# A vision-mamba pair on one core: stage openings, idle half units and turned sequences of the side work are rearranged

## The chip, the core and the metric

The kernel runs on one core of a Trainium2 chip. The metric is the time of one execution on the device, in microseconds (us). An engine's name is written as in the profile: PE (TensorE), DVE (VectorE), ACT (ScalarE), POOL (GpSimd), SP (SyncE, here the queue from which all DMAs are issued).

## The reference, cut to what matters

Eight images of 64 x 64 tokens with 192 channels go through two layers.

Layer 0 projects 192 channels to 2 x 384, applies a depthwise 3 x 3 convolution and silu to one half, runs a state-space scan over the tokens in two orders (along rows and along columns), gates the result with silu of the other half, projects back, adds the input, and adds an MLP (192 to 768 to 192).

Layer 1 splits the 192 channels in two halves. The left half goes through three convolutions. The right half is normalized, projected to 192 + 192, convolved depthwise, and scanned in four directions with 16 states per channel:

```python
def step(h, t):
    u_t, d_t, b_t, c_t = t
    h = jnp.exp(d_t[..., None] * A) * h + (d_t * u_t)[..., None] * b_t[:, :, None, :]
    return (h, jnp.einsum('bkdn,bkn->bkd', h, c_t))
scan_in = (jnp.moveaxis(xs4, -1, 0), jnp.moveaxis(delta, -1, 0), jnp.moveaxis(Bs, -1, 0), jnp.moveaxis(Cs, -1, 0))
...
_, ys = lax.scan(step, h0, scan_in)
ys = jnp.moveaxis(ys, 0, -1) + Ds[None, :, :, None] * xs4
...
yv = _ln(yv, out_norm_g, out_norm_b) * jax.nn.silu(z)
xr_out = jnp.einsum('bhwe,ce->bhwc', yv, out_proj_w)
```

Two of the four directions walk the tokens column by column ("turned" sequences), so a transposed copy of the scan's input is needed. The four results are added, normalized, gated and projected; both halves are interleaved and added to the layer's input.

## The kernel before, in words

The spine of the kernel is `selective_scan`, layer 1's scan. It runs 3072 units, 384 for each image. A unit is a tile of 128 rows (8 channels x 16 states) and 1024 tokens. For each unit SP fetches the decay's exponents (`fetch`, L1430, 512 KB, issued 6 units ahead), ACT takes their exponential (`decay`, L1435), PE spreads the input term over the states (`spread`, L1443), DVE multiplies by B (`weigh`, L1458) and scans (`scan`, L1465), POOL multiplies by C (L1467), ACT carries the last column on (L1473, L1474), and every fourth unit PE sums the states (`gather`, L1485). Each engine runs its instructions in the order in which the program emits them; `pin` keeps that order.

All other work runs beside the scan, in stages. They are Python generators, queued for each image: while image b is scanned, `conv0`, `ssd` and `mlp0` (layer 0) of image b+1 are emitted, then `conv_branch` with `scan_sums` as its side work and `scan_outputs` (end of layer 1) of image b-1, then `scan_inputs` and `transposed` (the inputs of the scan) of image b+1. Each unit has two halves, and in each half `Beside.half` emits some side work. A generator yields the cost of each piece in a rough unit, or `None`: wait for the next half. The credit rule is

```python
self.credit = min(self.credit, self.rate) + self.rate
while self.credit > 0.0 and self.stages:
    for cost in self.stages[0]:
        if cost is None:
            return
        self.credit -= cost
        if self.credit <= 0.0:
            return
    self.stages.pop(0)
```

and the rate is set once for each image from the sum of costs, the number of halves, and a reserve of 13 halves per stage (`spread_over`). Halves in which a stage only yields `None` are called empty here. The scan's own PE work also spends credit. What a stage has not emitted when its image's scan is about to end is emitted at once (`finish`); in both kernels nothing is left over there.

At its opening a stage loads what it needs. In `conv0` these are the first row of tokens, the projection weights `w_in`, the first block (`load(0)`), three parts of the convolution's diagonal weights (`diag`, L482), the projection `xp` (L486) and the second block. The second block is loaded twice, by two calls of `load(1)` into the same buffers; the second load is queued behind the first one's landing. `mlp0` loads `w_z`, the block's five tiles, `w_out` and `w1` before its first `gate`. `conv_branch` loads both convolutions' weights (L957), `scan_inputs` its two `diag` tiles (before the first `mean`). `ssd` opens with the steps of `group(0)`: loads, then POOL, ACT, POOL, PE and ACT, POOL in turn, with empty halves between them. `transposed` reads whole sequences (`whole`, L1100), copies each quarter with rows and columns exchanged on ACT (`part`, L1110), and stores it (L1117).

`stages(0)` runs before the scan with no scan beside it (the prologue), and the last image's sums and outputs run after it (the tail).

Of the kernel before, what the change touches and what calls it, by code (L numbers as in the profile page):

```python
# [9 lines left out]
F32 = mybir.dt.float32  # L10
# [7 lines left out]
L = HH * WW  # L18
# [271 lines left out]
def pause(n):  # L290

    for i in range(n):
        yield None


def among(gen, calls):

    calls = list(calls)
    for n, cost in enumerate(gen):
        yield cost  # L300
        if n % 2 == 1 and calls:
            calls.pop(0)()
    for call in calls:
        call()
        yield None
# [72 lines left out]
def conv0(cx, x):  # L378
# [3 lines left out]
    with cx.pool("cw0") as wp, cx.pool("v0", 2) as vp:  # L382
# [95 lines left out]

        pads = [wp.tile([128, R2 + 2, PW], F32, tag=f"pad{j}", name=f"pad{j}") for j in range(NJ)]
        diag = wp.tile([128, NJ, 9, 64], F32, tag="diag", name="diag")  # L480
        for j in range(NJ):
            pin(nc.sync.dma_start(out=diag[:, j], in_=k["diag0"][:, j]))  # L482
            yield None
        xp = wp.tile([128, 2 * NJ, 2 * NP0], F32, tag="xp0", name="xp0")
        for i in range(2):
            pin(nc.sync.dma_start(  # L486
                out=xp[64 * i : 64 * (i + 1)], in_=k["p0_xp"].rearrange("(j p) k m -> p j (k m)", p=64)
            ))
        yield from pause(2)
        for j in range(NJ):  # L490
            pin(nc.gpsimd.memset(pads[j], 0.0))
        yield from pause(2)
        load(1)
        yield from pause(2)
        load(1)
        for j in range(NJ):
            yield from project(0, j)
        for p in range(NP):
            for j in range(NJ):
                yield from convolve(p, j)  # L500
# [10 lines left out]
def ssd(cx):  # L511
# [15 lines left out]
    with cx.pool("g0", 2) as gp, cx.pool("s0", 2) as sp:  # L527
# [49 lines left out]
            groups[g] = both, over, *(t.rearrange(by_chunk, k=K2) for t in (dt, da, upto, toend))  # L577

        coming = group(0)
        for n in (8, 2, 2, 3, 2):  # L580
            next(coming)
            yield from pause(n)
        next(coming, None)
# [131 lines left out]
def mlp0(cx, x, x1):  # L715
# [9 lines left out]
    with cx.pool("mw0") as wp, cx.pool("m0", 2) as mp:  # L725
# [27 lines left out]
        def add(i):  # L753
            for y0, y1 in ys[i]:
                pin(nc.gpsimd.tensor_add(y0, y0, y1))
# [91 lines left out]
        w_out = wp.tile([128, NJ, C], F32, tag="w_out", name="w_out")  # L847
        w2 = wp.tile([128, NF, C], F32, tag="w2", name="w2")
        yield from load_split(cx, w_z, k["p0_w_in"][:, INNER0:])
        for call in loads(0):  # L850
            call()
            yield None
        pin(nc.sync.dma_start(out=w_out, in_=k["p0_w_out"].rearrange("(j p) m -> p j m", p=128)))
        yield None
        yield from load_split(cx, w1, k["p0_w1"])
        yield from gate(0)
        add(0)
        pin(nc.sync.dma_start(out=w2, in_=k["p0_w2"].rearrange("(f p) m -> p f m", p=128)))
        yield from turn(0)
        yield from project(0)  # L860
        for call in loads(1):
            call()
            yield None
        for i in range(1, NI + 1):
            if i < NI:
                yield from gate(i)
# [9 lines left out]
def conv_branch(cx, xl, short, out, side=None):  # L876

    nc, pin, k = cx.nc, cx.pin, cx.k
    with cx.pool("cw1") as wp, cx.pool("a1", 2) as ap:

        pads = [[wp.tile([CH, RB + 2, PW], F32, tag=f"p{c}{i}", name=f"p{c}{i}") for i in range(2)] for c in range(2)]
        xs, ys, os, shs, ws = {}, {}, {}, {}, []

        def conv(ps, pad, w):
            for t, (dy, dx) in enumerate(TAPS):
# [65 lines left out]
            yield 0.0  # L951

        load(0)
        for n in ("conv1_w", "conv2_w"):
            w = wp.tile([CH, 9, CH], F32, tag=n, name=n)
            for r in range(3):
                pin(nc.sync.dma_start(out=w[:, 3 * r : 3 * (r + 1)], in_=k[n][:, 3 * r : 3 * (r + 1)]))  # L957
                yield None
            ws.append(w)
# [50 lines left out]
def scan_inputs(cx, xr, xn, u):  # L1010
# [4 lines left out]
    with cx.pool("dw") as wp, cx.pool("b1", 2) as bp:  # L1015
# [71 lines left out]
        yield from in_turn(range(NB), mean, norm, project, wait, wait, convolve, store)  # L1087


def transposed(cx, u):  # L1090

    nc, pin = cx.nc, cx.pin
    with cx.pool("t1") as tp:
        wholes = []
        for n, src in enumerate((u[0], u[2][0:64])):
            wholes.append(tp.tile([src.shape[0], L], F32, tag=f"whole{n}", name=f"whole{n}"))

        def load(n, q):
            here = slice(q * L // 4, (q + 1) * L // 4)
            pin(nc.sync.dma_start(out=wholes[n][:, here], in_=(u[0], u[2][0:64])[n][:, here]))  # L1100

        for q in range(4):
            load(0, q)
            yield from pause(1 if q < 3 else 3)
        front = []
        for whole, dst in zip(wholes, (u[1], u[2][64:128])):
            for q in range(4):
                w0 = q * WW // 4
                part = tp.tile([whole.shape[0], L // 4], F32, tag="part", name="part", bufs=3)
                pin(nc.scalar.copy(part.rearrange("p (w h) -> p w h", h=HH), wh(whole)[:, w0 : w0 + WW // 4, :]))  # L1110
# [4 lines left out]
                yield None  # L1115
# [72 lines left out]
def scan_outputs(cx, y, xn, short, out):  # L1188
# [3 lines left out]
    with cx.pool("e1", 2) as ep:  # L1192
# [65 lines left out]
class Beside:  # L1258
# [465 lines left out]
```

## Time and profile before

| | us |
|---|---|
| median of 3 runs | 16537.61 (16530.31 to 16537.72) |
| the profiled execution's own time | 16556.29 |
| its span, first to last instruction | 16554.4 |
| prologue, to the first scan | 913 |
| image 0's scan | 1792 |
| image 1's and image 2's scan | 2004 and 2014 |
| image 7's scan | 1570 |
| tail | 264 |

The lower rows are read from the trace of the profiled execution by the start of each image's first scan instruction. All engines work in all of these stretches except the tail. In the profile a line such as L1465 is the line of the kernel that emitted the instruction, `h<-dA,carry,dB` names what it writes and reads, and the numbers behind the bar are busy us, mean ns of one, and idle us of the engine just before, with what ended it.

### The profile page before, as it was taken

How to read it: one execution, taken by the hardware profiler on the slowest of the kernel's cores; microseconds unless marked ns; L12 is line 12 of the kernel's file. 1: busy time of each engine (PE TensorE's matmuls, PEld its weight loads, DVE VectorE, ACT ScalarE, POOL GpSimd, SP SyncE). 2: the span in 40 equal slices, each digit the busy share in tenths (PEclk: the TensorE clock that was granted, in tenths of full speed). 3: DMA queues.
4: the chain of work that ended last, by engine and by line, in shares of the span. 5: the costliest groups of instructions: out<-in, count | busy, mean ns of one | idle time of the engine just before them, and what ended most of it. 6: DMA issues, size and time to landing. Idle time of an engine off the chain costs nothing.

```text
span 16554.4 us, 220424 instructions
## 1 busy us (share of the span) xinstructions
PE 13560.5 (82%) x75752; PEld 4803.7 (29%) x75752; DVE 12258.6 (74%) x9264; ACT 9901.5 (60%) x17354; POOL 10649.1 (64%) x5765
## 2 busy tenths in 40 slices
PE   8977887788977888888888789887898878878876
PEld 4423322332223321333213332233322333211111
DVE  2268888886778766887678876788767887778994
ACT  3365677565674656647566475665657556655653
POOL 3258766875568655686557865577655775566773
PEclk9987888889788896888878898788887889877766
DMA  3288878888787887888778878888778887788884
GB/s 90 84 218 198 214 196 227 194 209 202 182 226 192 202 208 184 222 193 207 205 195 208 199 199 207 206 202 198 196 195 212 200 209 203 193 224 201 214 209 125
DMA packets 1605044, 3248.22 MB, mean 196 GB/s; under 512 B 390536, under 2 KB 841752, under 8 KB 1603928
## 3 DMA queue, kind: packets, MB, share of 16 engines
q1 hardware_dynamic: 1603928, 3234.12, 78.5%
q8 instruction: 605, 9.91, 0.3%
q14 instruction: 511, 4.19, 0.1%
HBM read 2555.20 MB, written 678.18 MB: 195 GB/s over the span
## 4 chain that ended last, share of the span: by engine, by line
PE 41%; DMA 17%; DVE 16%; ACT 11%; POOL 8%; issue 5%; SPq 2%; DVEq 0%; POOLq 0%; ACTq 0%
DVE h L1465 9%; PE ps_cv L343 7%; DMA dA<-dld 5%; PE acc L1485 4%; DVE dB L1458 4%; PE ps_c L886 4%; POOL h L1467 3%; PE dB L1443 2%; ACT dA L1435 2%; PE ps_m L795 2%; PE ps_sum L1178 2%; PE ps_xp L1355 2%; DMA dus<-dud 2%; PE ps_y L686 1%; PE ps_var L1000 1%
## 5 line engine op out<-in xcount | busy, mean ns | idle before, releaser
L1467 POOL TENSOR_TENSOR h<-h,bc 128x1023 f32<-128x1023 f32 x3072 | 7229.2, 2354 | 4661.0 <-DVE h L1465 4123.4
L1465 DVE TENSOR_TENSOR_SCAN h<-dA,carry,dB 128x1024 f32<-128x1024 f32 x3072 | 7201.5, 2344 | 712.6 <-ACT dA L1435 224.1
L1458 DVE TENSOR_TENSOR dB<-dB,bc 128x1024 f32<-128x1024 f32 x3072 | 3742.3, 1218 | 1921.2 <-PE dB L1443 1909.4
L1435 ACT ACTIVATE dA<-dA,neg_a 128x1024 f32<-128x1024 f32 x3072 | 3505.9, 1141 | 44.2 <-DMA dA<-dld 39.1
L1485 PE MATMUL acc<-h,gather 128*32 128x512 f32 x12288 | 2310.3, 721 | 524.3 <-ACT h L1474 230.7
L1443 PE MATMUL dB<-dus,spread 24*128 24x512 bf16 x6144 | 1379.8, 434 | 849.4 <-DVE h L1465 764.0
L1490 ACT COPY y<-acc 128x512 f32<-128x512 f32 x1536 | 883.3, 575 | 944.0 <-PE acc L1485 818.5
L886 PE MATMUL ps_c<-p,conv_w 96*96 96x512 f32 x2304 | 1242.8, 668 | 70.2 <-ACT p L906 63.2
L1443 PEld LDWEIGHTS <-spread 24*128 24x128 bf16 x6144 | 309.6, 93 | 3099.6 <-issue 1452.3
L1473 ACT COPY carry<-h 128x1 f32<-128x1 f32 x3072 | 573.0, 187 | 947.5 <-DVE h L1465 944.4
L686 PE MATMUL ps_y<-dtx,M 64*64 64x64 f32 x12288 | 784.9, 258 | 333.6 <-DVE Hn L677 309.4
L1474 ACT ACTIVATE h<-h,bc 128x1 f32<-128x1 f32 x3072 | 905.2, 295 | 158.7 <-ACT carry L1473 3.0
L343 PE MATMUL ps_cv<-pad,diag 64*64 64x512 f32 x6912 | 835.6, 603 | 6.4 <-ACT y L1490 5.4
L686 PEld LDWEIGHTS ps_y<-dtx,M 64*64 64x64 f32 x12288 | 662.5, 169 | 492.7 <-issue 311.4
L1485 PEld LDWEIGHTS acc<-h,gather 128*32 128x32 f32 x12288 | 304.6, 117 | 1535.5 <-issue 938.2
L107 ACT ACT_TABLE_LOAD x577 | 740.3, 1283 | 10.2
L618 PE MATMUL ps_d<-R,after 128*128 128x384 f32 x1024 | 565.0, 642 | 72.5 <-POOL R L594 26.9
L613 ACT COPY bc<-ps_t 64x256 f32<-64x256 f32 x256 | 93.4, 365 | 855.9 <-PE ps_t L608 855.6
L886 PEld LDWEIGHTS ps_c<-p,conv_w 96*96 96x96 f32 x2304 | 368.5, 177 | 777.8 <-issue 686.8
L1355 PE MATMUL ps_xp<-u,xp 128*108 128x512 f32 x768 | 474.4, 706 | 98.9 <-DMA u<-u 86.1
L1394 POOL TENSOR_TENSOR du<-dl,u 128x1024 f32<-128x1024 f32 x192 | 452.2, 2355 | 127.0 <-ACT dl L1391 127.0
L373 PE MATMUL ps_h<-oa,w1a 128*128 128x256 f32 x1536 | 451.5, 414 | 58.6 <-ACT h L826 17.3
(243 smaller groups left out, 19239.9 us busy)
## 6 DMA issues: line engine op xcount, KB each, us to landing
dA<-dld SPq DMA_DIRECT2D x3072, 512.0 KB
dud<-terms SPq DMA_DIRECT2D x192, 768.0 KB
dus<-dud SPq DMA_DIRECT2D x2304, 64.0 KB
bc<-bcd SPq DMA_DIRECT2D x256, 512.0 KB
y<-yrows SPq DMA_DIRECT2D x256, 384.0 KB
u<-u SPq DMA_DIRECT2D x192, 512.0 KB
dld<-dl SPq DMA_DIRECT2D x192, 512.0 KB
y<-y SPq DMA_DIRECT2D x3072, 32.0 KB
```

Source lines behind the costliest of these rows:

```text
L343: pin(nc.tensor.matmul(ps[64 * b : 64 * (b + 1)].rearrange("p (h w) -> p h w", w=WW), lhsT=diag[:, t, :], rhs=pad[64 * i : 64 * (i + 1), b ...
L686: pin(nc.tensor.matmul(psy[d][here, h * HP : (h + 1) * HP], lhsT=M[here, d, h, :], rhs=dtx[here, d, h, :], start=True, stop=d == 1,))
L886: pin(nc.tensor.matmul(ps.rearrange("p (h w) -> p h w", w=WW), lhsT=w[:, t, :], rhs=pad[:, dy : dy + RB, dx : dx + WW], start=t == 0, stop ...
L1355: pin(nc.tensor.matmul(ps[:NXP], lhsT=k["xp"][:, g, t, :], rhs=u_of[m][t][:, here], start=t == 0, stop=t == 2))
L1435: pin(nc.scalar.activation(dAs[q], dAs[q], AF.Exp, scale=k["neg_a"][:, steps[m][1], t, i : i + 1]))
L1443: pin(nc.tensor.matmul(dBs[q][:, half, :], lhsT=k["spread"][at : at + 3 * UD, :], rhs=du_of[n][at : at + 3 * UD, i // 2, :], start=True, s ...
L1458: pin(nc.vector.tensor_mul(dBs[q], dBs[q], of(q)[0]))
L1465: pin(nc.vector.tensor_tensor_scan(order(h, g), order(dA, g), order(dB, g), carry, ALU.mult, ALU.add))
L1467: pin(nc.gpsimd.tensor_mul(h[:, rest], h[:, rest], C_[:, rest]))
L1474: pin(nc.scalar.activation(end, end, AF.Identity, scale=C_[:, last : last + 1]))
L1485: pin(nc.tensor.matmul(ps[32 * v : 32 * (v + 1)], lhsT=k["gather"], rhs=hs[q - 3 + v][:, here], start=True, stop=True))
L1490: pin(nc.scalar.copy(y[:, here], ps))
```

## The change

- `among` gets a parameter `n`: a call is made after every n-th piece (it was every second).
- `conv0` loads only the first part of `diag` ahead of its first pieces. The other two parts and `xp` are loaded among the first projections, one after each piece. The doubled `load(1)` is a single one, behind those projections. Fewer empty halves.
- `ssd` opens with 7, 1, 1, 2, 1 empty halves in place of 8, 2, 2, 3, 2.
- `mlp0` starts `gate(0)` when x and half of y are loaded. The rest of y and `w_out` come among its pieces, `w1` after it, and `w2` among the pieces of `project(0)` with the next block.
- `conv_branch` loads the second convolution's weights among its first pieces.
- `scan_inputs` loads its `diag` tiles among its first pieces, and has 4 empty halves for 6; `scan_outputs` has 4 for 6.
- `transposed` copies two quarters in each half in place of one, with four `part` buffers in place of three, and starts one half earlier.
- The reserve in `spread_over` is 9 halves per stage in place of 13.

```diff
-def among(gen, calls):
+def among(gen, calls, n=2):
     calls = list(calls)
-    for n, cost in enumerate(gen):
+    for i, cost in enumerate(gen):
         yield cost
-        if n % 2 == 1 and calls:
+        if i % n == n - 1 and calls:
             calls.pop(0)()
...
# conv0
-        for j in range(NJ):
+        def load_diag(j):
             pin(nc.sync.dma_start(out=diag[:, j], in_=k["diag0"][:, j]))
-            yield None
-        xp = wp.tile([128, 2 * NJ, 2 * NP0], F32, tag="xp0", name="xp0")
-        for i in range(2):
...
+        load_diag(0)
         yield from pause(2)
         for j in range(NJ):
             pin(nc.gpsimd.memset(pads[j], 0.0))
-        yield from pause(2)
+        yield from pause(1)
+        for j, calls in enumerate(([lambda: load_diag(1)], [lambda: load_diag(2)], [load_xp])):
+            yield from among(project(0, j), calls, 1)
         load(1)
-        yield from pause(2)
-        load(1)
-        for j in range(NJ):
-            yield from project(0, j)
...
# ssd
-        for n in (8, 2, 2, 3, 2):
+        for n in (7, 1, 1, 2, 1):
...
# mlp0
-        for call in loads(0):
-            call()
-            yield None
-        pin(nc.sync.dma_start(out=w_out, in_=k["p0_w_out"].rearrange("(j p) m -> p j m", p=128)))
+        first, *calls = loads(0)
+        first()
...
+        calls.pop(0)()
         yield None
+        calls.pop(0)()
+        yield from pause(2)
+        yield from among(gate(0), calls + [load_out], 1)
+        yield None
+        add(0)
         yield from load_split(cx, w1, k["p0_w1"])
-        yield from gate(0)
-        add(0)
-        pin(nc.sync.dma_start(out=w2, in_=k["p0_w2"].rearrange("(f p) m -> p f m", p=128)))
         yield from turn(0)
-        yield from project(0)
-        for call in loads(1):
-            call()
-            yield None
+        yield from among(project(0), loads(1) + [load_2], 1)
...
# conv_branch
+        for r in range(3):
+            load_w(0, r)
+            yield None
         load(1)
...
-        yield from in_turn(range(NB), scale, first, wait, second, third, add, store)
+        turns = in_turn(range(NB), scale, first, wait, second, third, add, store)
+        yield from among(turns, [lambda r=r: load_w(1, r) for r in range(3)])
...
# scan_inputs
-            pin(nc.sync.dma_start(out=diag[n], in_=k["diag_" + n]))
-            yield from pause(2)
-        yield from pause(2)
+        yield from pause(4)
...
+        yield from among(turns, [
+            lambda n=n: pin(nc.sync.dma_start(out=diag[n], in_=k["diag_" + n])) for n in "ab"
+        ])
...
# transposed
-            yield from pause(1 if q < 3 else 3)
+            yield from pause(1 if q < 3 else 2)
...
-                part = tp.tile([whole.shape[0], L // 4], F32, tag="part", name="part", bufs=3)
+                part = tp.tile([whole.shape[0], L // 4], F32, tag="part", name="part", bufs=4)
...
-                yield 1.0
-                yield None
+                if q % 2 == 1:
+                    yield 1.0
+                    yield None
...
# scan_outputs
-                yield from pause(6)
+                yield from pause(4)
...
# Beside.spread_over
-        self.rate = own / halves + work / (halves - 13 * len(self.stages))
+        self.rate = own / halves + work / (halves - 9 * len(self.stages))
```

More of the change, by code (lines that the diff above doesn't have):

```diff
@@ L480, in conv0, with load_xp @@
         diag = wp.tile([128, NJ, 9, 64], F32, tag="diag", name="diag")
-        for j in range(NJ):
+        xp = wp.tile([128, 2 * NJ, 2 * NP0], F32, tag="xp0", name="xp0")
+        def load_diag(j):
             pin(nc.sync.dma_start(out=diag[:, j], in_=k["diag0"][:, j]))
-            yield None
-        xp = wp.tile([128, 2 * NJ, 2 * NP0], F32, tag="xp0", name="xp0")
-        for i in range(2):
-            pin(nc.sync.dma_start(
-                out=xp[64 * i : 64 * (i + 1)], in_=k["p0_xp"].rearrange("(j p) k m -> p j (k m)", p=64)
-            ))
+        def load_xp():
+            for i in range(2):
+                pin(nc.sync.dma_start(
+                    out=xp[64 * i : 64 * (i + 1)], in_=k["p0_xp"].rearrange("(j p) k m -> p j (k m)", p=64)
+                ))
+        load_diag(0)
         yield from pause(2)
@@ L849, in mlp0, with load_out, load_2 @@
         yield from load_split(cx, w_z, k["p0_w_in"][:, INNER0:])
-        for call in loads(0):
-            call()
-            yield None
-        pin(nc.sync.dma_start(out=w_out, in_=k["p0_w_out"].rearrange("(j p) m -> p j m", p=128)))
-        yield None
+        first, *calls = loads(0)
+        first()
+        def load_out():
+            pin(nc.sync.dma_start(out=w_out, in_=k["p0_w_out"].rearrange("(j p) m -> p j m", p=128)))
+        def load_2():
+            pin(nc.sync.dma_start(out=w2, in_=k["p0_w2"].rearrange("(f p) m -> p f m", p=128)))
+        calls.pop(0)()
+        yield None
+        calls.pop(0)()
[3 more added lines that the diff above has]
+        add(0)
         yield from load_split(cx, w1, k["p0_w1"])
-        yield from gate(0)
-        add(0)
-        pin(nc.sync.dma_start(out=w2, in_=k["p0_w2"].rearrange("(f p) m -> p f m", p=128)))
         yield from turn(0)
-        yield from project(0)
-        for call in loads(1):
-            call()
-            yield None
+        yield from among(project(0), loads(1) + [load_2], 1)
         for i in range(1, NI + 1):
@@ L881, in conv_branch @@
         pads = [[wp.tile([CH, RB + 2, PW], F32, tag=f"p{c}{i}", name=f"p{c}{i}") for i in range(2)] for c in range(2)]
-        xs, ys, os, shs, ws = {}, {}, {}, {}, []
+        xs, ys, os, shs = {}, {}, {}, {}
         def conv(ps, pad, w):
@@ L953, in conv_branch, with load_w @@
         load(0)
[L954 to L957, printed above, removed]
-                yield None
-            ws.append(w)
+        ws = [wp.tile([CH, 9, CH], F32, tag=n, name=n) for n in ("conv1_w", "conv2_w")]
+        def load_w(i, r):
+            here = slice(3 * r, 3 * (r + 1))
+            pin(nc.sync.dma_start(out=ws[i][:, here], in_=k[("conv1_w", "conv2_w")[i]][:, here]))
+        for r in range(3):
+            load_w(0, r)
+            yield None
         load(1)
@@ L1086, in scan_inputs @@
                 pin(nc.gpsimd.memset(pads[n][i], 0.0))
-        yield from in_turn(range(NB), mean, norm, project, wait, wait, convolve, store)
+        turns = in_turn(range(NB), mean, norm, project, wait, wait, convolve, store)
+        yield from among(turns, [
+            lambda n=n: pin(nc.sync.dma_start(out=diag[n], in_=k["diag_" + n])) for n in "ab"
+        ])
 def transposed(cx, u):
@@ L1113, in transposed @@
                     load(1, q)
-                yield 1.0
-                yield None
+                if q % 2 == 1:
+                    yield 1.0
+                    yield None
                 if len(front) == 2:
```

## The prediction

> **What bounds the kernel now.** I read the page's engine rows first. TensorE (PE) is busy 82%, VectorE 74% and the 16 DMA engines 78.5%: no engine is full, so the limits differ by stage. One scan unit costs VectorE 2344 + 1218 ns (rows L1465, L1458), so no unit can take under 3.56 us.
>
> ```profile
> span 16554.4 us, 220424 instructions
> ...
> PE 13560.5 (82%) x75752; PEld 4803.7 (29%) x75752; DVE 12258.6 (74%) x9264; ACT 9901.5 (60%) x17354; POOL 10649.1 (64%) x5765
> ...
> q1 hardware_dynamic: 1603928, 3234.12, 78.5%
> ...
> L1465 DVE TENSOR_TENSOR_SCAN h<-dA,carry,dB 128x1024 f32<-128x1024 f32 x3072 | 7201.5, 2344 | 712.6 <-ACT dA L1435 224.1
> L1458 DVE TENSOR_TENSOR dB<-dB,bc 128x1024 f32<-128x1024 f32 x3072 | 3742.3, 1218 | 1921.2 <-PE dB L1443 1909.4
> ```
>
> Second, the busy times by stretch, cut at the borders of the stages that run beside image 2's scan, and one stretch of the last image with no side work. The columns are the stretch, its length, busy us of PE, PE loads, VectorE, ScalarE, GpSimd, then granted clock, DMA share and GB/s.
>
> ```profile
> 4610.00:4914.00 304.00, 270.84 (x1916) 100.05 (x1914) 250.29 (x142) 221.75 (x412) 199.22 (x100) 0.93 0.91 231
> 4914.00:5461.00 547.00, 418.43 (x4000) 193.04 (x4000) 452.85 (x449) 263.25 (x503) 455.49 (x287) 0.80 0.80 189
> ...
> 5901.00:6196.00 295.00, 270.16 (x753) 75.31 (x750) 187.58 (x107) 139.80 (x255) 164.33 (x90) 0.95 0.85 218
> 6196.00:6361.00 165.00, 144.27 (x288) 30.61 (x286) 111.57 (x91) 119.16 (x186) 95.17 (x50) 0.65 0.69 167
> 6361.00:6563.00 202.00, 185.71 (x760) 43.74 (x762) 153.34 (x99) 133.54 (x226) 113.04 (x59) 0.76 0.73 183
> 6563.00:6613.00 50.00, 17.76 (x52) 2.04 (x46) 24.63 (x15) 31.10 (x37) 22.96 (x11) 0.53 0.87 245
> ...
> 6624.00:6665.00 41.00, 27.56 (x78) 8.07 (x78) 24.88 (x15) 14.58 (x29) 21.28 (x12) 0.67 0.96 220
> ...
> 15975.00:16290.00 315.00, 169.26 (x556) 25.29 (x552) 301.76 (x175) 181.05 (x336) 232.95 (x102) 0.62 0.80 192
> ```
>
> In order: conv0, ssd, conv_branch, scan_outputs, scan_inputs, transposed, the opening of the next conv0, bare scan. The same stretches restricted to L1465 hold 71, 96, 53, 25, 41, 7, 7 and 87 scans, so a unit takes 4.28, 5.70, 5.57, 6.60, 4.93, 7.14, 5.86 and 3.62 us. The reader is to see three things. Bare scan runs at VectorE's bound. conv_branch (PE 92% busy) and conv0 (89%) are at TensorE. The two stretches around the image change have TensorE below 70% and DMA at 0.87 and 0.96: they wait for transfers.
>
> Third, the chain of waits in the 120 us around that image change (start, length, what):
>
> ```profile
> 6579.37 15.45 DMA dA<-dld
> 6596.64 7.02 DMA whole<-u
> 6603.81 1.99 ACT part L1110
> ...
> 6619.77 8.18 DMA dud<-terms
> 6627.96 10.40 DMA w_inb<-in_w_in_dram
> 6638.43 5.77 DMA dA<-dld
> ...
> 6650.08 8.73 DMA diag<-diag
> 6658.84 10.27 DMA y<-y
> ```
>
> Transfers end these waits, one of them the diag load that the change moves.
>
> **The change, part by part.** I sum against the profiled execution, 16556.29 us with 16554.4 of span. That is 18.7 us (0.11%) above the median of 16537.61; I carry the sum over as a difference.
>
> *(A) Fewer empty halves, smaller reserve (13 to 9 per stage).* I walked the credit rule of `half` through all 6144 halves with both sets of yields. Opening halves in which a stage issues no compute fall: conv0 12 to 6, ssd 16 to 11, mlp0 9 to 4, conv_branch 6 to 3, scan_outputs 5 to 3, scan_inputs 5 to 3. The rate falls too, 2.305 to 2.231 credits a half. So the work does not close up much: halves per stage are conv0 143 to 144, ssd 192 to 189, mlp0 175 to 175, conv_branch 107 to 106, scan_outputs 50 to 48, scan_inputs 81 to 80, transposed 14 to 9, idle before the next image 6 to 17. Halves that spend no credit at all: 224 to 221 of 768. What is saved at the openings is handed back as a longer idle end. Upper bound of the gain, if each unit keeps its stage's pace and the freed ones run at 3.6: 1.5 x 2.1 (ssd) + 0.5 x 1.97 + 1 x 3.0 + 0.5 x 1.33 - 0.5 x 0.68 (conv0) = 7.5 us an image. Lower bound 0: the same matmuls must pass a TensorE that is 90% busy. I take the middle, 4 us, x 6 images: -24.
>
> *(B) The doubled load(1) of conv0 goes.* Before issues xa (512 KB) and two xb (64 KB) twice into the same buffers, the second time queued on SP behind the landing of the first. 640 KB at the 231 GB/s of that stage is 2.8 us, with DMA 91% busy. Seven conv0 stages run beside a scan: -20. In the first one (94 GB/s, no scan) it is free.
>
> *(C) Two diag loads and xp go behind the first projections.* 2 x 288 KB + 430 KB = 1.0 MB leave the stretch at 0.96 DMA share. 7 scans took 41 us there against 25 at 3.6: 16 us lost, 8.73 of them in the chain under diag. The bytes return under conv0 at 0.91, so the bounds are 0 and -16; I take -7, x 7: -49. The earlier end of transposed (8.5 units before the image switch, where 3 were) is the same slack, not counted again.
>
> *(D) Turned sequences in pairs.* Eight L1110 copies take 1.94 us each on ScalarE. Two per half instead of one leaves their sum, 15.6 us; ScalarE's scan work meanwhile (dA 1142, two carry pieces 183 and 295, y and terms, some 2.75 a unit) is only spread over fewer units. The first copy comes one half earlier, and it waits for the last `whole` load, issued at 6578.63 and used at 6589.89, 11.3 us later. That landing doesn't move, so ScalarE stops one half (1.8 us) sooner and the dA activations behind it stand: +1.8, x 7: +13. A fourth `part` buffer gains nothing while the `u<-part` stores share a DMA at 245 GB/s. Bounds: -8.9 (2.5 units at 7.14 become 3.6) to +4.
>
> *(E) Shorter leads.* First pieces now follow their loads by about 4 halves (7.2 us at scan pace), in mlp0 by 2 (3.6 us). PE, ScalarE and GpSimd run in order, so a first matmul that waits for its load holds the next `spread` behind it (L1443), and VectorE waits for that. The trace before doesn't show these waits: its leads were 7 to 12 halves. Nearest row: the 11.3 us of `whole` above, and 10.40 for w_inb in the chain. A wait is at least 0, at most some 4 us at each of five openings. [...] +5 an image, x 7: +35. ssd's steps of one half (GpSimd add, softplus, multiply, matmul) are in this: each waits one engine earlier than before.
>
> *(F) Cold openings.* The granted clock falls to 0.53 in transposed and 0.62 in bare scan; conv_branch's first eight matmuls take a median of 1061 ns where all of L886 have 592. [...] One would hope that shorter openings save this price, some 8 x 0.47 = 3.8 us at each of five openings, 19 us an image. [...] I take 0.
>
> The prologue and the last image gain nothing that I can price: in `finish` the yields have no effect, and image 7 has 176 idle halves already (184 after). Weights among the first pieces (conv2_w, diag a/b, w1, w2, w_out) are moved on SP past dA fetches, same count and bytes: 0 beyond (C).
>
> Sum: -24 - 20 - 49 + 13 + 35 = -45 us, 0.27%: 16537.6 - 45 = 16493.
>
> **The rivals.** A measurement of this kernel can tell about 0.2%, 33 us, from no change.
>
> *Rival 1, the openings pay in full.* (A) 7.5 x 6, (B) 20, (C) 10 x 7, with (D) and (E) at 0, and a third of (F)'s 19 x 6 = 38: -173, 16365. For it: the chain above is all transfers. Against it: unchanged zero-credit halves.
>
> *Rival 2, nothing.* Idle moves to the end, bytes move 20 us later under a DMA at 0.91, and -24 - 20 is eaten by (D) and (E): within 33 us, 16520.
>
> *Rival 3, slower: the first pieces wait in order.* Where the loads take 11 us, as `whole` did, leads of 4 halves miss by 4 us. Five openings an image x 4 x 7 = +140, with (B) and (C) at -69 and (D) +13: +84, 16622. It decides once loads land more than some 9 us after issue. For it: DMA shares of 0.85 to 0.96. Against: after (C) the opening queues are shorter than those that showed 11 us.
>
> **How the numbers follow.** Forecast (-33 to -110) 0.36, rival 1 0.14, rival 2 0.22, rival 3 0.28. Faster 0.50, same 0.22, slower 0.28. The side pieces meet other units than before, and 8 to 11 us stalls recur at fixed units in each image; that shuffling has no sign and widens everything. The range leaves out the far half of rivals 1 and 3: 16375 to 16630. The forecast's own range is 16425 to 16505.
>
> **What would show it.** Right: the conv0 opening (41 us) shorter by 5 to 10 us and no diag in its chain; the end of each image a longer stretch at 3.6 us a unit; transposed still about 45 to 50 us with its first copy waiting longer. Wrong: first matmuls L373 or L886, or GpSimd's y add, ending waits for DMA of several us at openings (rival 3); stage times of ssd and conv_branch off by more than 10 us each, which my terms don't hold.

## The result: slower by 0.75%, and the profile after

The changed kernel takes 16649.76 us (median of 4 runs, 16632.21 to 16672.08). The kernel before, run beside it, takes 16533.96 us (4 runs, 16500.32 to 16537.72). The ratio is 1.0075, with a 95% interval of 1.0056 to 1.0094. The prediction was 16493 us, range 16375 to 16630, with 0.50 for faster. It was wrong, and on the wrong side.

The head of the page of the changed kernel, in the order of the lines shown of before:

```profile
span 16630.4 us, 220292 instructions
...
PE 13487.7 (81%) x75752; PEld 4816.2 (29%) x75752; DVE 12225.6 (74%) x9264; ACT 9923.3 (60%) x17373; POOL 10658.2 (64%) x5765
...
q1 hardware_dynamic: 1601496, 3227.83, 77.9%
...
L1478 DVE TENSOR_TENSOR_SCAN h<-dA,carry,dB 128x1024 f32<-128x1024 f32 x3072 | 7199.9, 2344 | 836.8 <-ACT dA L1448 266.5
L1471 DVE TENSOR_TENSOR dB<-dB,bc 128x1024 f32<-128x1024 f32 x3072 | 3734.9, 1216 | 1930.8 <-PE dB L1456 1923.3
```

No engine's work accounts for the loss (VectorE is busy 12225.6 us, before 12258.6, and PE 72.8 less; ScalarE works 21.8 us longer and GpSimd 9.1), and q1 moves 6.3 MB less, which is the second load of conv0's block (768 KB, eight times). The span is 76 us longer all the same. For VectorE all of it is waiting: its idle ahead of the scan rises from 712.6 to 836.8 us.

The stretches beside image 2's scan, at this kernel's own stage borders (same columns as before: length, PE, PE loads, VectorE, ScalarE, GpSimd, granted clock, DMA share, GB/s); in order conv0, ssd, conv_branch, scan_outputs, scan_inputs, transposed, the idle end, and the opening of the next conv0:

```profile
4662.00:4962.00 300.00, 265.91 (x1902) 99.33 (x1900) 239.54 (x137) 223.67 (x411) 187.44 (x92) 0.92 0.88 216
4962.00:5506.00 544.00, 413.17 (x3978) 193.93 (x3978) 445.33 (x443) 252.85 (x489) 451.44 (x285) 0.79 0.77 186
5956.00:6252.00 296.00, 278.76 (x762) 77.41 (x760) 187.45 (x107) 140.88 (x256) 164.95 (x90) 0.93 0.86 218
6252.00:6400.00 148.00, 121.95 (x288) 27.51 (x280) 107.07 (x89) 114.25 (x179) 90.06 (x48) 0.73 0.74 179
6400.00:6580.00 180.00, 170.39 (x770) 40.60 (x766) 149.91 (x98) 133.67 (x226) 114.18 (x60) 0.83 0.81 208
6580.00:6616.00 36.00, 8.76 (x24) 1.33 (x21) 13.69 (x9) 14.41 (x17) 10.38 (x5) 0.57 0.84 210
6616.00:6660.00 44.00, 20.71 (x63) 2.99 (x64) 31.65 (x19) 31.51 (x49) 26.78 (x12) 0.58 0.76 217
6660.00:6700.00 40.00, 27.68 (x100) 8.94 (x100) 21.37 (x13) 15.31 (x32) 17.59 (x11) 0.87 0.86 192
```

transposed and the opening stand out: in 36 us VectorE works 13.69, in the 40 us of the opening 21.37. Stage borders move by up to 11 halves between the two kernels, so I compare by scan unit instead. The table is worked out from the starts of L1478 (L1465): the mean over images 1 to 6, summed over four stretches (us an image).

| kernel | units 0 to 51: rest of conv0 | 52 to 348: ssd to scan_inputs | 349 to 362: transposed, idle end | 363 to 383: next opening | sum |
|---|---|---|---|---|---|
| before | 216.8 | 1619.5 | 73.9 | 92.4 | 2002.6 |
| after | 227.4 | 1610.8 | 84.7 | 93.7 | 2016.6 |
| difference | +10.6 | -8.7 | +10.8 | +1.3 | +14.0 |

Six such images make 84 us; with image 0 at +16, image 7 at +6, the prologue at +1 and the tail at -32 that is the 76 us of the span (rounded). The tail's -32 us is no gain of the change. Its work is the same, at a granted clock of 0.77 here and 0.64 before; b_once, which has the old code there, takes 230 us for it at 0.75. Without the tail the loss is 108 us, near the 116 us between the medians. It has two main places. The second, transposed, is in the chain of waits at the image change (start, length, what):

```profile
6585.17 4.96 DMA dus<-dud
...
6595.45 11.34 DMA whole<-u
6606.93 3.73 ACT part L1122 x2
6611.08 6.55 DMA whole<-u
6617.73 3.77 ACT part L1122 x2
...
6672.81 6.76 DMA xa<-in_x_dram
6679.70 3.75 PE ps_in L373 x4
...
6690.33 0.34 PE dB L1456 x2
6690.70 1.24 DVE dB L1471
```

The last `whole` load of the first sequence takes 11.34 us from issue to use, as before; ACT now reaches its copy sooner and stands there longer. These are the waits around that copy, before and after (who waited for what, us in total, times, longest):

```profile
ACT part L1110 <- DMA dA<-dld: 15.9, 1, 15.9
DVE h L1465 <- ACT dA L1435: 14.7, 1, 14.7
```

```profile
DVE h L1478 <- ACT dA L1448: 21.9, 1, 21.9
ACT part L1122 <- DMA whole<-u: 21.1, 1, 21.1
```

The shorter lead of conv0 is there too: four L373 matmuls behind a load of 6.76 us. But that stretch lost 1.3 us an image, not more.

The first place is not an opening at all. This is what ACT waited for ahead of `po<-ps_p`, the copy in `turn` whose buffer is freed by the store `prows<-po` (instructions by tile, us and times; the kernel before first, then the changed one):

```profile
its engine sat idle before it (us, times) until:
  DMA prows<-po: 93.8, 23
```

```profile
its engine sat idle before it (us, times) until:
  DMA prows<-po: 198.2, 27
```

That is +104.4 us over seven conv0 stages beside a scan, 14.9 an image, in code that the change does not touch. The waits are longer (7.3 us for 4.1 in the mean) more than they are frequent. The timeline of one of them in the changed kernel (start, length, engine, line; unit 16 beside image 1), ACT first, then SP's queue:

```profile
2790.94 0.45 ACT L467 COPY po<-ps_p 128x140 f32<-128x140 f32 x2 [0.74 <-PE ps_p L460]
...
2793.32 0.30 ACT L1487 ACTIVATE h<-h,bc 128x1 f32<-128x1 f32 x1
2803.12 0.45 ACT L467 COPY po<-ps_p 128x140 f32<-128x140 f32 x2 [9.51 <-DMA prows<-po]
```

```profile
2785.91 1.26 SPq L1432 DMA_DIRECT2D dus<-dud  x2
2787.27 0.52 SPq L1443 DMA_DIRECT2D dA<-dld  x1
2787.83 0.59 SPq L397 DMA_DIRECT2D xa<-in_x_dram  x1
...
2792.83 0.37 SPq L472 DMA_DIRECT2D prows<-po  x1
2794.69 0.52 SPq L1443 DMA_DIRECT2D dA<-dld  x1
```

Every 16 units the scan starts a new tile, for which SP issues twelve `dus` loads, most of them in units 9 to 13 of the tile before. Here the turn falls just behind them and behind two 512 KB loads, and ACT goes on only at 2803.12, 10.3 us after the store was issued. The waits of those 15 us show who pays:

```profile
DVE dB L1471 <- PE dB L1456: 10.2, 1, 10.2
ACT po L467 <- DMA prows<-po: 9.5, 1, 9.5
PEld ps_p L460 <- ACT po L467: 9.0, 1, 9.0
```

ACT stands, PE stands behind ACT, the next `spread` behind that on PE, and VectorE behind `spread`: unit 16 takes 15.9 us as the median of images 1 to 6, before 3.9 (with 13.1 for unit 17).

### The profile page after: what moved, and what is told of

The parts are those of the page before. It is cut to its first block, busy times and chain, and to the rows that moved or that the text cites. A ratio compares the mean times of both kernels' runs of the same rounds, so it can differ in the third digit from the quotient of the medians.

```text
span 16630.4 us, 220292 instructions
## 1 busy us (share of the span) xinstructions
PE 13487.7 (81%) x75752; PEld 4816.2 (29%) x75752; DVE 12225.6 (74%) x9264; ACT 9923.3 (60%) x17373; POOL 10658.2 (64%) x5765
## 4 chain that ended last, share of the span: by engine, by line
PE 30%; DVE 16%; DMA 13%; ACT 10%; POOL 9%; issue 5%; SPq 2%; DVEq 0%; ACTq 0%; POOLq 0%
DVE h L1478 10%; PE ps_cv L343 5%; DVE dB L1471 4%; PE acc L1498 4%; POOL h L1480 3%; DMA dA<-dld 3%; PE ps_c L893 3%; ACT dA L1448 2%; PE dB L1456 2%; PE ps_sum L1191 2%; DMA dus<-dud 1%; PE ps_xp L1368 1%; DMA prows<-po 1%; PE ps_m L797 1%; DMA out_dram<-o 1%
## 5 line engine op out<-in xcount | busy, mean ns | idle before, releaser
L1478 DVE TENSOR_TENSOR_SCAN h<-dA,carry,dB 128x1024 f32<-128x1024 f32 x3072 | 7199.9, 2344 | 836.8 <-ACT dA L1448 266.5
L1471 DVE TENSOR_TENSOR dB<-dB,bc 128x1024 f32<-128x1024 f32 x3072 | 3734.9, 1216 | 1930.8 <-PE dB L1456 1923.3
L1456 PE MATMUL dB<-dus,spread 24*128 24x512 bf16 x6144 | 1375.3, 434 | 690.9 <-DVE h L1478 618.2
L1456 PEld LDWEIGHTS <-spread 24*128 24x128 bf16 x6144 | 309.9, 93 | 2971.0 <-issue 1442.9
L620 PE MATMUL ps_d<-R,after 128*128 128x384 f32 x1024 | 600.7, 679 | 81.1 <-POOL R L596 40.7
L373 PE MATMUL ps_h<-oa,w1a 128*128 128x256 f32 x1536 | 466.5, 425 | 73.2 <-ACT y L1503 43.0
```

The source lines that it names most:

```text
L1456: pin(nc.tensor.matmul(dBs[q][:, half, :], lhsT=k["spread"][at : at + 3 * UD, :], rhs=du_of[n][at : at + 3 * UD, i // 2, :], start=True, s ...
L1471: pin(nc.vector.tensor_mul(dBs[q], dBs[q], of(q)[0]))
L1478: pin(nc.vector.tensor_tensor_scan(order(h, g), order(dA, g), order(dB, g), carry, ALU.mult, ALU.add))
```

## The experiments

Ratios are to the kernel before, run on the same chip in the same session, with 95% intervals. The theories as I held them at first: *short lead* (first pieces wait for their loads), *bandwidth* (bytes at the opening count), *shifted phase* (which scan units a piece meets sets what it costs). *Store buffer* (the po wait) came from the second session.

**First session: each suspected part alone, and each short lead undone.**

t_lead: `yield from pause(1 if q < 3 else 2)` becomes `pause(1 if q < 3 else 8)` behind the `whole` loads of the changed kernel.

> The changed kernel, with 8 empty halves in place of 2 between the last load of the first whole sequence and the first turned copy; every other piece of every stage stays in its half. In the changed kernel's trace the first copy waits 21.1 us for its load at each image change, and VectorE idles 21.9 us behind it. Short-lead theory: 6 more halves (10.8 us of scan) take most of that wait away; unit 352 falls from 26.5 us to below 12 us, 10 us are saved at each of 7 image changes, 70 us in all: about 16580. Bandwidth theory (the transfers around the image change are the bound, so the wait only moves): within 20 us of the changed kernel, 16630 to 16670. Shifted-phase theory (the loss lies in other units that each piece meets): no part of the loss is here, same 16630 to 16670.

Measured: 1.0053 (1.0039 to 1.0067), 16605.07 us. Units 349 to 362 go back from 84.7 to 75.2 us. So transposed's lead is a real part, about 0.2%, and no more.

c_lead: ahead of conv0's first projections in the changed kernel

```diff
-        yield from pause(1)
+        yield from pause(6)
```

> The changed kernel, with 6 empty halves in place of 1 between conv0's loads and its first projection. In the changed kernel's trace the first matmul on xa waits 6.9 us at a cold clock and unit 365 takes 21.2 us. Short-lead theory: that unit falls to below 10 us, 7 image changes x 10 us: 16580. Bandwidth theory: no change, 16650. Shifted-phase theory: later stages move by up to 4 halves, so their times change by more than 5 us an image each, with either sign; the total lies anywhere within 80 us of 16650.

Measured: 0.9943 (0.9929 to 0.9957), 16418.72 us: five empty halves turn the change into a gain. That looked like a triumph of the short-lead theory. By stretches it is not: against the changed kernel -11.7 us an image in units 0 to 51, -19.4 in 52 to 348, -7.8 in transposed, and only -2.4 at the opening itself. No theory had room for a gain of 231 us. (The cold clock of the expectation, in the changed kernel's trace: behind a wait of 6.94 us the granted clock is 0.50 from 6679 to 6684 us, and four L373 matmuls take 3.75 us; the next four of that shape, at 1.00, take 1.98.)

b_turned: the kernel before with the new `transposed` alone.

> The kernel before, with the new transposed alone (pairs of copies, four buffers, one empty half less). Short-lead theory: the stretch of transposed and the idle halves behind it lose 7 to 11 us an image against before, 50 to 80 us in all: 16590 to 16610. My prediction's term (1.8 us an image) would give 16550. Shifted-phase theory: conv0 starts at the same unit as before and no other stage moves by more than 2 halves, so about 16535 to 16550.

Measured: 1.0026 (1.0012 to 1.0039). Pairs with the short lead lose by themselves.

b_conv0: the kernel before with the new opening of conv0 alone.

> The kernel before, with the new opening of conv0 alone (one load of the second block, two diag parts and xp behind the first projections, 6 empty halves in place of 12). Short-lead theory: unit 365 takes about 20 us as in the changed kernel, and the conv0 stage at the pace of bare scan for its extra units loses about 10 us an image: 16600. My prediction's terms (doubled load and diag) would give a gain of 60 us: 16475. Shifted-phase theory: between 16480 and 16600, with changes in ssd and later stages of more than 5 us.

Measured: 1.0064 (1.0050 to 1.0078). The conv0 opening can make nearly the whole loss; ACT's idle ahead of po is 168.8 us here, against 93.8.

**Second session: is it the lead, or where the rest comes to stand?**

bc_lead: b_conv0 with `pause(6)`.

> The kernel before with the change's conv0 opening (single second block, two diagonal parts and xp behind the first projections) but with five empty halves put back ahead of the projections, so that their lead is the old one. Short-lead theory: the loss of the conv0 opening alone (ratio 1.0064) was the lead, so it goes: ratio 0.998 to 1.002, conv0's time over 3.6 us a unit back from 60.9 to 47 to 49 us. Bandwidth theory (the megabyte that left the opening and the load not made twice are worth what the prediction gave them, 69 us, once the lead doesn't eat it): ratio 0.995 to 0.997. Shifted-phase theory (loss and gain come from which units meet which pieces): the stages stand within one half of where they stood before, so ratio 0.999 to 1.001, whatever the loads.

Measured: 1.0025 (1.0014 to 1.0035). The lead returns 0.4%, but the bytes moved away from the opening are no gain: units 363 to 383 take 94.6 us (before 92.4), units 0 to 51 take 222.2 (216.8), and the idle ahead of po is 147.1 us. The bandwidth theory falls here. The other two are missed as well (at most 1.002 and 1.001): with the lead and nearly all positions of before, the new opening of conv0 still costs something.

a_shift: the changed kernel, lead untouched, with the halves behind conv0's last piece:

```diff
             for q in range(4):
                 yield from turn(p, q)
+        yield from pause(5)
```

> The changed kernel with the same five empty halves, but behind conv0's last piece and not ahead of its first projections: every later stage stands where it stands with the long lead (within one half), the lead stays short. The long lead had made the changed kernel 231 us faster than its own median. Short-lead theory: nothing of that returns here, ratio to the kernel before 1.006 to 1.009, conv0 61 us over 3.6 a unit. Shifted-phase theory: what came in ssd, mlp0, scan_inputs and the end of the image (some 130 of the 231 us) returns, conv0's 98 us don't: ratio 0.999 to 1.001. Bandwidth theory has no change against the changed kernel: 1.007.

Measured: 0.9950 (0.9930 to 0.9970), 16454.25 us. This is the run that decided most. Openings, loads and leads are those of the changed kernel; conv0 waits as there (a_shift, instructions by tile):

```profile
its engine sat idle before it (us, times) until:
  DMA prows<-po: 202.7, 29
```

and still the kernel is faster than before. Units 52 to 348 fall from 1610.8 to 1587.5 us. The short-lead theory had no place for that; shifted phase had (it gave 0.999 to 1.001, too little).

One rival has to be weighed. The five halves also put conv0's last stores further from ssd's first loads. c_lead has no such gap. Over 3.6 us a unit, mlp0 takes 13 us an image less than in the changed kernel in both runs, and scan_inputs 11 less (a_shift) and 12 less (c_lead): that much goes with position. ssd takes 11 less in a_shift and 5 in c_lead, so there the gap may have a part.

both_lead: c_lead and t_lead together.

> The changed kernel with both leads back: five empty halves ahead of conv0's projections and six more halves behind the last whole load of transposed. Short-lead theory: the two gains add (231 us and 45 us): ratio 0.991 to 0.993, 16375 us. Shifted-phase theory: the end of the image is moved once more and can go either way: 0.990 to 0.998. Bandwidth theory: as with conv0's lead alone, 0.994.

Measured: 0.9928 (0.9909 to 0.9947). The two nearly add; the idle ahead of po is down to 55.5 us.

b_late: the kernel before with the new openings of conv_branch, scan_outputs and scan_inputs alone.

> The kernel before with the changed openings of conv_branch, scan_outputs and scan_inputs alone. Short-lead theory: their leads of 3 to 4 halves are paid too, up to 4 us each: ratio 1.001 to 1.005, and conv_branch's time over 3.6 us a unit goes up from 106 us. Bandwidth theory: w2's half and the diagonal tiles leave the openings: 0.997 to 1.000. Shifted-phase theory: conv0 and ssd as before, the late stages change by up to 10 us in either direction: 0.996 to 1.004.

Measured: 0.9948 (0.9930 to 0.9966). The shorter leads cost nothing that shows; the edit as a whole gains. It also moves scan_inputs and transposed to other units, and the two are not told apart. Another miss for the short-lead theory.

**Third session: take the wait away.** A third buffer, with room made from xc:

```diff
-            po = vp.tile([128, 2, 2 * NP0], F32, tag="po", name="po")
+            po = vp.tile([128, 2, 2 * NP0], F32, tag="po", name="po", bufs=3)
...
-                xc = ... tag="xc", name="xc", bufs=7)
+                xc = ... tag="xc", name="xc", bufs=6)
```

a_po3 has it in the changed kernel, b_po3 in the kernel before, both_po3 in both_lead. The smaller xc adds no wait that shows: ACT's idle ahead of the copy into xc is 101.5 us for the convolution in the changed kernel, and 101.2 in a_po3.

> The changed kernel with three po buffers instead of two (and six xc buffers instead of seven, to make room). In the changed kernel's trace ACT idles 198.2 us ahead of po copies for the stores prows<-po, in the kernel before 93.8 us. Store-buffer theory (conv0's turn pieces now fall where SP is busy with the scan's own issues, so the store that frees po lands late, ACT stands in front of a po copy, and the scan stands behind ACT): that idle falls under 60 us and units 0, 16 and 48 of an image (13.4, 15.9, 11.0 us) fall under 8 us; ratio to the kernel before 0.996 to 1.001. Short-lead theory (the openings are the loss): nothing changes, 1.006 to 1.009. Next-in-line theory (with po free the next thing behind SP is late, the scan's own du and decay fetches): the idle goes, the units stay over 10 us, 1.003 to 1.008.

Measured: 1.0046 (1.0033 to 1.0059), and between the theories. The wait for prows is gone, unit 48 falls from 11.0 to 4.2 us, but units 0 and 16 only to 10.8 and 13.0. The copy to the neighbouring tile xo, whose three buffers were free in time before (4.7 us of idle, none for its store), now waits (a_po3, instructions by tile):

```profile
its engine sat idle before it (us, times) until:
  DMA xrows<-xo: 131.8, 18
```

So 198.2 us of one wait became 131.8 of the next in line: the store-buffer theory had the place right, the next-in-line theory the size (though it took the scan's own fetches for the next in line, and not xo).

> The kernel before with three po buffers instead of two (and six xc buffers instead of seven). Store-buffer theory: most of its 93.8 us of idle ahead of po goes, unit 17 (13.1 us) falls to under 6: ratio 0.994 to 0.998. Short-lead theory says nothing of it: 0.998 to 1.002. Next-in-line theory: 0.998 to 1.002, with another wait at unit 17.

Measured: 0.9944 (0.9932 to 0.9956). In the kernel before, the same buffer takes the whole wait ahead of po away, and only 32.7 us appear ahead of xo; unit 17 falls from 13.1 to 3.6 us.

> The changed kernel with both leads back (five empty halves ahead of conv0's projections, six behind the last whole load of transposed), and three po buffers instead of two (six xc). With the leads alone 55.5 us of idle ahead of po are left. Store-buffer theory: some 30 to 40 us of them go: ratio 0.990 to 0.992, 16350 to 16390 us. Next-in-line theory: as with the leads alone, 0.993. Short-lead theory: 0.993.

Measured: 0.9897 (0.9881 to 0.9912), 16366.67 us: the best version of all. No store wait is left at po; at xo 18.5 us are.

b_once: the kernel before with one `load(1)` instead of two.

> The kernel before with the second block of conv0 loaded once and not twice; empty halves as before. The prediction priced this step at 20 us (2.8 us at each of seven openings). If bytes at the opening are what counts: ratio 0.998 to 0.999. If the double load lay beside other work: 0.9995 to 1.0005. If the time of SP's queue counts (the second load waited behind the landing of the first, and what SP issues next stood behind it): 0.994 to 0.998.

Measured: 0.9985 (0.9976 to 0.9994), about 25 us (10 to 40 by the interval). That is what bytes at the opening would give.

**Fourth session: phase, and whether parts add.**

a_shift2: `pause(2)` in place of a_shift's `pause(5)`.

> The changed kernel with two empty halves behind conv0's last piece, where five had given ratio 0.995. Openings and conv0 are as in the changed kernel; mlp0 and all that follows stand where they stand with five (two halves later than in the changed kernel), ssd starts two halves later and not five. Shifted-phase theory (which scan units a piece meets sets what it costs): mlp0 to the end of the image gain as with five, ssd takes any place between: 0.994 to 1.001. Short-lead theory: 1.006 to 1.009. Store-buffer theory: conv0's waits are the changed kernel's, which alone gives no gain: 1.006 to 1.009.

Measured: 0.9963 (0.9951 to 0.9975). Two empty halves are enough. What mlp0 takes over 3.6 us a unit is 117 and 118 us an image in the two shifted kernels, and 130 in the changed one, for the same pieces begun two halves earlier. The gap ahead of ssd remains a rival for ssd alone, which takes 11 us less here too.

b_shift5: the kernel before with `pause(5)` behind conv0.

> The kernel before with five empty halves behind conv0's last piece; no opening, load or buffer is touched. Shifted-phase theory: moves by over 0.2% in some direction, 0.990 to 1.008. Short-lead theory and store-buffer theory: nothing but the packing of the rest (two halves fewer of slack at the end): 0.999 to 1.003.

Measured: 1.0019 (1.0009 to 1.0030). The same edit on the kernel before loses a little. Inside it much moves and cancels: over 3.6 us a unit mlp0 takes 15 us an image more and conv_branch 18 more, scan_outputs 10 and scan_inputs 21 less. A change of the whole by over 0.2% is not shown here, and the ratio lies where the theories that expect nothing had it. A dependence of each stage on its position is shown.

b_rest: the kernel before with the new openings of ssd and mlp0 and the reserve of 9.

> The kernel before with what no run has taken alone yet: the changed openings of ssd and mlp0 and the reserve of 9 halves per stage. The parts measured alone make +0.64% (conv0), +0.26% (turned), -0.52% (conv_branch, scan_outputs, scan_inputs), and the whole is +0.75%. If the parts add, this one is +0.37%: ratio 1.002 to 1.005. If they do not (shifted-phase theory), anything from 0.994 to 1.006. Short-lead theory: ssd's and mlp0's shortened steps are paid at up to 4 us each: 1.001 to 1.004.

Measured: 0.9956 (0.9941 to 0.9972). With the smaller rate conv0's turns move too, and the idle ahead of po is 35.0 us. The parts taken alone make +0.64, +0.26, -0.52 and -0.44%, in sum -0.06%; together they make +0.75%.

b_combo: b_po3, b_late and b_once together.

> The kernel before with what helped alone: three po buffers (0.9944), the changed openings of conv_branch, scan_outputs and scan_inputs (0.9948), and the second block loaded once (0.9985). None of them moves another's stage by a half. If they add: 0.987 to 0.989, 16310 us, faster than the best so far (0.9897). Shifted-phase theory: the same, since conv0, ssd and mlp0 stand where they stood. Next-in-line theory (what one frees the next one takes): 0.991 to 0.994.

Measured: 0.9930 (0.9912 to 0.9947), where the sum of the three is -1.23%. The gains do not add either. The next-in-line theory gave this range; shifted phase, which had them add, missed it.

## Why the prediction was wrong, step by step

| step | predicted us | measured |
|---|---|---|
| A, fewer empty halves | -24 | not apart from the rest; units 52 to 348: -8.7 an image, 6 images: -52 |
| B, second load of conv0 | -20 | b_once: -25 (-10 to -40) |
| C, diag and xp behind the projections | -49 | bc_lead less b_once, with `load(1)` moved too: +0.40%, +66 |
| D, pairs of parts | +13 | b_turned: +0.26%, +43 |
| E, shorter leads | +35 | PE's wait for conv0's first block: 0 before, 41.9 after; worth some 17 to 43 |
| not in the sum: pieces meet other units | 0, "no sign" | a_shift2: two empty halves give -198; ACT idle ahead of po: +104 |

**The step that failed first is the one left out of the sum.** The text said that the side pieces meet other units than before and that "that shuffling has no sign and widens everything". It was put at 0, and moved alone it is larger than the whole forecast sum of -45 us: two empty halves behind conv0 (a_shift2), with every load and opening of the change in place, take the median from 16649.76 to 16451.26 us. The prediction's own counts of halves let mlp0 start 2 halves earlier than before, scan_inputs 5 and transposed 6. By the same walk c_lead, a_shift and a_shift2 bring these three back to within one half of where they stood, and then the kernel is 0.4 to 0.6% faster than before. This suggests, without proving it, that the forecast failed less on what the openings are worth than on what they displace.

The wait that shows this best is po's. Its +104 us are idle time of ACT; taking them away (a_po3) returned 52 us of the kernel's time, since xo waited next. It could have been priced in part: the kernel before showed 93.8 us of ACT idle ahead of po, unit 17 at 13.1 us, and the walk through the credit rule gave the new position of every turn. Setting those positions against the 16-unit rhythm of SP's `dus` loads would have shown the first turns moving just behind them. From the trace (issue of a `prows` store to the last of its completions, median by unit of issue): in the changed kernel 10.5 us at unit 383, 10.9 at 15, 9.9 at 46; in c_lead, with the turns two to three units later, 7.2 at unit 2, 6.6 at 18, 6.7 at 48. How much of the +104 us belongs to one early start and how much to the bytes put behind the projections is not separated: b_conv0 (168.8) and bc_lead (147.1) have both in different shares.

**C had the wrong sign.** The opening was priced by its DMA share of 0.96 and the 8.73 us of diag in its chain. With diag gone from there, the chain held another load nearly as long (xa, 6.76 us), and the stretch took no less (94.6 us in bc_lead, 93.3 in b_once, 92.4 before). The same bytes then lie where conv0's stores are, and the idle ahead of po is 147.1 us in bc_lead against 96.8 in b_once; that the bytes cause it is argued, not shown. Here the 8.73 us of a load in the chain were not worth their length, since one of 6.76 us stood beside it.

**D was mis-sized.** One half earlier was taken as 1.8 us. The copy does wait longer, as the prediction said, but by 5.2 us (21.1 against 15.9), and VectorE by 7.2 (21.9 against 14.7). Units 349 to 362 lost 3.3 us in b_turned and 10.8 in the changed kernel; six halves of lead take 9.5 of them back.

**E came at one opening, not at five.** Predicted: first pieces wait up to 4 us at five openings, +5 us an image in all. PE's waits for the input blocks beside the scan, the kernel before first, then the changed one (us in total, times, longest; `ps_in` is conv0's projection, `ps_z` the gate of mlp0):

```profile
PE ps_z L373 <- DMA xa<-in_x_dram: 42.7, 7, 7.4
```

```profile
PE ps_in L373 <- DMA xa<-in_x_dram: 41.9, 7, 7.7
PE ps_z L373 <- DMA xb<-in_x_dram: 33.0, 7, 5.7
```

conv0's first matmuls wait 6 us at each opening, where they had not waited, and hold PE: in the chain above the next `spread` (L1456) comes at 6690.33, behind them, and VectorE's L1471, which waits for it, at 6690.70, after 17.42 us of idle; in mlp0 the wait is about what it was (33.0 us, and 7.7 more for xa). With conv0's lead restored the wait is gone, and the stretch of the opening is 2.4 us an image shorter (c_lead against the changed kernel) or 6.2 (bc_lead against b_conv0, 100.8 to 94.6): times 7, some 17 to 43 us. So the term was near in size, by one larger wait in place of five small ones. The trace before had held such waits, in mlp0, though the prediction says that it shows none. The three late openings with shorter leads gained as a whole (b_late). In transposed a longer lead is worth t_lead's 0.2%. For conv0, c_lead alone (0.9943) seems to prove that it is worth far more, and a_shift (0.9950 with the short lead) shows why one should not read it so: most of what the lead brought came with moving what follows.

**A has the sign that was taken, but not by its reasoning.** The stretch it spoke of is 8.7 us an image shorter, where 4 were taken and 7.5 was the bound; five empty halves behind conv0 take another 23.3 us from it. An agreement within a phase effect nearly three times as large is no confirmation. **B** was right in mechanism, and its size agrees within a wide interval. Its bytes were read wrongly: conv0's two xb loads are 128 KB each (the 64 KB are mlp0's), so one second load is 768 KB, 3.4 us at 231 GB/s, and seven are -24 us. **F** (no gain from shorter idle) was an estimate. The trace before shows slow matmuls at a low granted clock (conv_branch's first eight: a median of 1061 ns, at 0.55 from 5915 to 5922 us; 592 ns for all of L886), but how much idle time brings them is not shown. No run tests F by itself; the mean granted clock is 0.828, before 0.831, which does not speak against it.

**The rivals.** Rival 3 gave 16622 us, nearest to the measured time, but its mechanism, first pieces in order behind late loads, is not what cost the time: the wait came anew at conv0's opening alone, where it is worth some 17 to 43 us and not 140. That its number is near is luck. Two of the signs of being wrong did come: L373 waits for DMA of several us, and ssd takes 11 us an image more over 3.6 us a unit, which no term held.

**What stays open.** Which of the pieces in mlp0 and the stages behind it meet what at their two positions (12 us an image in mlp0 alone) is not resolved to single waits. That it is position and not code is shown for mlp0 and scan_inputs by a_shift, a_shift2 and c_lead together; for ssd, position and the gap ahead of it are not separated.

## What to carry to other kernels

Where side work is laid by a credit rule beside a main loop, an edit to an opening moves everything behind it; before pricing the edit, set the new positions against the main loop's own rhythm of DMA issues, and look for unchanged copies that wait for their buffer's store. Test a lead with a control that adds the same empty slots elsewhere: if that helps as much, the lead is not shown. Before counting on slots, remove the waits that depend on position: here a third store buffer with both leads restored made 1.03% out of a change that had lost 0.75%.

## What was not expected of the hardware

The landing of one and the same 140 KB store is not one figure: the median is 4.9 us before and 4.8 after, but the slowest tenth takes over 7.2 us before and over 10.0 after. Of the 13 over 10.0 us after, 12 were issued at units 382, 383, 15 and 46, the last two units of a tile of 16 and so just behind the `dus` loads for the next; that these loads are the cause is not shown by a run. A single such store was a stop for three engines: at unit 16 beside image 1 ACT stood 9.5 us, PE 8.8 behind it and VectorE 10.2 behind PE. And these stops are regular: unit 16 took 15.9 us as the median of six images, so that what looked like noise in the mean of a stage was a fixed place in the schedule.
